# Pairwise bilinear interaction: x turned by 16 transposes a tile with straight and crosswise copies in place of 32, and three parts of w in one buffer

## The chip, the core and the metric

The kernel runs on one core of one Trainium2 chip. The metric is device time in microseconds (us) of one execution. Before the change the median of four runs is 1346.43 us (1346.36 to 1346.82).

## The reference

x (called r_inputs) holds 4,096 samples of 32 fields of 64 numbers; w holds one 64x64 matrix for each of the 496 pairs of fields i < j. All is float32. Cut to what matters:

```python
F = inputs.shape[1]                                  # 32
idx_i, idx_j = np.triu_indices(F, k=1)               # 496 pairs, i < j
vi = inputs[:, idx_i, :]                             # (4096, 496, 64)
vj = inputs[:, idx_j, :]
vidots = jnp.einsum('bpd,pde->bpe', vi, W)           # W: (496, 64, 64)
return vidots * vj                                   # (4096, 496, 64) float32
```

So for every sample and pair the field vector x_i is multiplied by the pair's own matrix, and the result element by element by x_j. The inputs are 42 MB, the output is 520 MB.

## The kernel before, in words

**Tiles and steps.** The samples are cut into 16 blocks of 256 rows, and each block into two tiles of 128 rows, a row to a partition: 32 tiles. A tile is computed in 46 steps. A step belongs to one field i and takes up to 16 of its pairs (CH), which lie side by side in w's order: its result, 128 rows by 16 pairs by 64, fills a PSUM buffer of two banks. Steps are bundled in five groups of 90 to 105 pairs (bounds, L45), and each group collects its products in one SBUF buffer `ot`, of which there are three. When a group is complete, SyncE (SP) issues one output transfer for it (L266), of 2.9 to 3.4 MB.

**A step on the engines.** TensorE (PE) multiplies x of field i, turned so that its 64 numbers lie along the partitions (`xT`), by the turned w of the pairs (`wT`), in two matmuls, h = 0 and h = 1, for the two halves of the 64 output columns (L244). Both use 64 partitions: the halves of `wT` for the two h lie on partitions 0 to 63 and 64 to 127, so field i's turned x is needed on the lower 64 partitions for h = 0 and on the upper 64 for h = 1. Where a step's pairs cross from one part of w to the next (at pairs 128, 256 and 384), it takes four matmuls. VectorE (DVE) then multiplies the result by x of the fields j and writes `ot` (L261). For the first step of the fields 1, 3, ... 13 (`aside`) ScalarE (ACT) copies the result to `tmp` instead (L258), and GpSimd (POOL) multiplies (L259).

**Turning x.** `turn_x` (L138) turns eight fields of a tile at a time (RUN), so four times a tile. The x buffer of a block has 65 slots of 64 columns: one of zeros in front, set by POOL (L72), and 64 for the fields of the two tiles. Each transpose takes two neighbouring slots, 128 rows by 128 columns: after it field n-1 lies on the lower partitions and field n on the upper ones. One transpose is done for every field, eight a turn (L143), into a PSUM buffer `ptx`, and one ACT copy of 128x1024 takes them to `xT` (L147). A step of field i then reads its lower half from the transpose of field i+1 and its upper half from that of field i (L243, L246). So the turn of fields 8q to 8q+7 is first needed by the steps of field 8q-1.

**Turning w.** The 496 matrices are loaded in three parts of 128 and one of 112 (`load_w`, L113); the first two borrow `ot` buffers and the fourth reuses the third's. Each part is put in order in four pieces (`order_w`, L120, on DVE, POOL or ACT) and turned on PE (`turn_w`, L127), and each turned piece is copied to the part's own buffer wT (L136). Part 0 is turned ahead of the first step, the others between steps.

**Order of the work.** The program runs through one list of steps (`sched`, L167). The first three tiles (LEAD) run group by group, all three through group 0, then through group 1, and so on, so that work can begin while parts of w are still to be turned; the other 29 tiles run one after the other. A table of due places (L176 to L187) says ahead of which step each turn stands: that of x stands AHEAD = 4 places before the first step that reads it. On each engine the instructions run in the order in which the program issues them. Four PSUM buffers are shared by the steps and by all turns; there are four buffers for xT and four for tmp, which also holds the ordered w.

**Loading x.** Block 0 is loaded in two halves (one per tile) and block 1 in one piece, all by SP among the first loads of w: block 0's first half, w parts 0 and 1, block 0's second half, w part 2, block 1 (L193 to L200). Later blocks are loaded at the seventh step (LATE = 6) of the block before, by ACT's queue, and every third one by `load_fifteen` (L95): 120 rows by two transfers that POOL issues, each followed by a tiny one to the buffer `scratch` (L92), and the last 8 rows by ACT.

Of the kernel before, what the change touches and what calls it, by code (L numbers as in the profile page):

```python
# [8 lines left out]
F32 = mybir.dt.float32  # L9
# [3 lines left out]
def kernel(  # L13
# [16 lines left out]
    nc = tc.nc  # L30

    B, F, D = x.shape
    P = 128
    NB = 2
# [3 lines left out]
    E2 = D // 2  # L38
    BANK = 512
    CH = BANK // E2  # L40
    RUN = 2 * BANK // P
    p0 = [i * (F - 1) - i * (i - 1) // 2 for i in range(F)]


# [7 lines left out]
    wrows = list(zip(cuts[:-1], cuts[1:]))  # L52

    const = ctx.enter_context(tc.tile_pool(name="const", bufs=1))
    xpool = ctx.enter_context(tc.tile_pool(name="xpool", bufs=2))
    xtpool = ctx.enter_context(tc.tile_pool(name="xtpool", bufs=4))
    tpool = ctx.enter_context(tc.tile_pool(name="tpool", bufs=4))
    opool = ctx.enter_context(tc.tile_pool(name="opool", bufs=3))
    psum = ctx.enter_context(tc.tile_pool(name="psum", bufs=4, space=bass.MemoryType.PSUM))

    ident = const.tile([P, P], F32, tag="ident", name="ident")
    make_identity(nc, ident)

    xs = {}

    def rows_of(dram: bass.AP, blk: int) -> bass.AP:
        return dram[blk * NB * P : (blk + 1) * NB * P]

    def new_x(blk: int):

        xs[blk] = xpool.tile([P, 1 + NB * F, D], F32, tag="xs", name=f"xs_{blk}")
        nc.gpsimd.memset(xs[blk][:, 0, :], 0.0)  # L72

    def load_x(blk: int, eng, k0: int = 0, k1: int = NB):
        src = rows_of(x, blk).rearrange("(p k) f d -> p (k f) d", k=NB)
        eng.dma_start(out=xs[blk][:, 1 + k0 * F : 1 + k1 * F, :], in_=src[:, k0 * F : k1 * F, :])

# [8 lines left out]
    def turn_engines(k: int):  # L86
        n = k if k > 1 else 17
        c = used[0] % 8
        used[0] += 1
        src = x[: NB * n].rearrange("(p k) f d -> p k f d", k=NB)  # L90
        tc.keep_in_program_order(
            nc.gpsimd.dma_start(out=scratch[:n, :, c : c + 1], in_=src[:, :, 0, 0:1])  # L92
        )

    def load_fifteen(blk: int):  # L95
        rows = rows_of(x, blk).rearrange("(p k) f d -> p k f d", k=NB)
        dst = xs[blk][:, 1:, :].rearrange("p (k f) d -> p k f d", k=NB)
        for a, b in ((SWR, SWR + 5), (SWR + 5, P)):
            nc.scalar.dma_start(out=xs[blk][a:b, 1:, :], in_=rows[a:b].rearrange("p k f d -> p (k f) d"))
        for h in range(2):  # L100
            cut = slice(h * F // 2, (h + 1) * F // 2)
            tc.keep_in_program_order(
                nc.gpsimd.dma_start(out=dst[:SWR, :, cut, :], in_=rows[:SWR, :, cut, :])  # L103
            )
            turn_engines(1)
# [3 lines left out]
    raw, wT = {}, {}  # L109
    EU = 2 * BANK // P  # L110
    NU = E2 // EU

    def load_w(c: int, eng=nc.sync):  # L113

        a, b = wrows[c]
        pool, tag = ((opool, "ot"), (opool, "ot"), (const, "w3"), (const, "w3"))[c]
        raw[c] = pool.tile([P, D * D], F32, tag=tag, name=f"raw_{c}")
        eng.dma_start(out=raw[c][: b - a, :], in_=wflat[a:b])

    def order_w(c: int, k: int, copy):  # L120
        r = wrows[c][1] - wrows[c][0]
        rp = tpool.tile([P, EU, 2, D], F32, tag="tmp", name=f"rp_{c}_{k}")
        src = raw[c][:r, :].rearrange("p (d h e) -> p e h d", h=2, d=D)
        copy(rp[:r], src[:, k * EU : (k + 1) * EU])  # L124
        return rp

    def turn_w(c: int, k: int, rp, copy):  # L127
        r = wrows[c][1] - wrows[c][0]
        if c not in wT:
            wT[c] = const.tile([P, r, E2], F32, tag=f"w{c}", name=f"wT_{c}")  # L130
        pt = psum.tile([P, EU, P], F32, tag="ps", name=f"ptw_{c}_{k}")
        for n in range(EU):
            nc.tensor.transpose(  # L133
                pt[:, n, :r], rp[:r, n].rearrange("p h d -> p (h d)"), ident[:r, :r]
            )
        copy(wT[c][:, :, k * EU : (k + 1) * EU], pt[:, :, :r].rearrange("p e r -> p r e"))  # L136

    def turn_x(blk: int, k: int, q: int, copy):  # L138

        pt = psum.tile([P, RUN, P], F32, tag="ps", name=f"ptx_{blk}_{k}_{q}")  # L140
        for n in range(RUN):
            s = k * F + q * RUN + n
            nc.tensor.transpose(  # L143
                pt[:, n, :], xs[blk][:, s : s + 2, :].rearrange("p f d -> p (f d)"), ident
            )
        xT = xtpool.tile([P, RUN, P], F32, tag="xT", name=f"xT_{blk}_{k}_{q}")
        copy(xT, pt)  # L147
        return xT


# [8 lines left out]
    first = {}  # L159
# [11 lines left out]
    place = {ts: n for n, ts in enumerate(sched)}  # L171


    AHEAD = 4
    due: dict = {}
    for t in range(NT):  # L176
        for q in range(F // RUN):
            at = place[t, first[q * RUN - 1] if q else 0] - AHEAD
            due.setdefault(max(0, at), []).append(("x", t // NB, t % NB, q))
    for c, orders, turns in (  # L180
# [10 lines left out]
    loads[place[LEAD, LATE]] = 2  # L191

    new_x(0)  # L193
    load_x(0, nc.sync, 0, 1)
    load_w(0)
    load_w(1)
    load_x(0, nc.sync, 1, NB)
    load_w(2)
    new_x(1)
    load_x(1, nc.sync)  # L200
    turn_engines(5)

    v, p, a = nc.vector.tensor_copy, nc.gpsimd.tensor_copy, nc.scalar.copy
    xT, rps = {}, {}
    xT[0, 0, 0] = turn_x(0, 0, 0, a)
    due[0] = [d for d in due[0] if d != ("x", 0, 0, 0)]
    for k, copy in enumerate((v, v, v, a)):
        rps[0, k] = order_w(0, k, copy)
    for k, copy in ((0, a), (3, a), (1, v), (2, a)):
        turn_w(0, k, rps.pop((0, k)), copy)  # L210

    ots = {}
    for s, (t, st) in enumerate(sched):
        blk, kt = divmod(t, NB)
        g, i, c0, m = steps[st]
        if s in loads:
            new_x(loads[s])
            if loads[s] % 3 == 1:
                load_fifteen(loads[s])
            else:  # L220
                load_x(loads[s], nc.scalar)
        for what, *args in due.get(s, ()):
            if what == "x":
                xT[tuple(args)] = turn_x(*args, a)
            elif what == "turn":
                turn_w(*args, rps.pop(tuple(args)), a)
            else:
                c, k = args
                rps[c, k] = order_w(c, k, (v, v, p, v)[c] if k % 2 == 0 else (v, v, p, a)[c])
                if (c, k) == (2, NU - 1):  # L230
                    load_w(3, nc.scalar)

        base, end = groups[g]
        pa = p0[i] + c0
        if pa == base:
            ots[t] = opool.tile([P, cap, D], F32, tag="ot", name=f"ot_{t}_{g}")
        ot = ots[t]
        ps = psum.tile([P, 2, CH, E2], F32, tag="ps", name=f"ps_{s}")
        for c, (lo, hi) in enumerate(wrows):
            lo, hi = max(pa, lo), min(pa + m, hi)  # L240
            if lo < hi:
                for h in range(2):
                    n = i + 1 - h  # L243
                    nc.tensor.matmul(  # L244
                        ps[:, h, lo - pa : hi - pa, :],
                        xT[blk, kt, n // RUN][h * D : (h + 1) * D, n % RUN, :],  # L246
                        wT[c][h * D : (h + 1) * D, lo - wrows[c][0] : hi - wrows[c][0], :],
                        start=True,
                        stop=True,
                    )  # L250
        o = pa - base
        j = 1 + kt * F + i + 1 + c0
        dst = ot[:, o : o + m, :].rearrange("p m (h e) -> p m h e", h=2)
        src = ps[:, :, :m, :].rearrange("p h m e -> p m h e")
        xj = xs[blk][:, j : j + m, :].rearrange("p m (h e) -> p m h e", h=2)
        if i in aside and c0 == 0 and s not in no_aside:
            tmp = tpool.tile([P, CH, 2, E2], F32, tag="tmp", name=f"tmp_{s}")
            nc.scalar.copy(tmp, src)  # L258
            nc.gpsimd.tensor_mul(dst, tmp, xj)  # L259
        else:  # L260
            nc.vector.tensor_mul(dst, src, xj)  # L261

        ends = (p0[2], end) if s < NS and (t, g) == (0, 0) else (end,)
        if pa + m in ends:
            n0 = p0[2] if len(ends) > 1 and pa + m == end else base
            nc.sync.dma_start(  # L266
                out=rows_of(out, blk).rearrange("(p k) n d -> p k n d", k=NB)[:, kt, n0 : pa + m, :],
                in_=ot[:, n0 - base : pa + m - base, :],
            )
# [28 lines left out]
```

## Time and profile before

| | before |
|---|---|
| median of 4 runs | 1346.43 us (1346.36 to 1346.82) |
| the profiled execution: its time | 1346.36 us |
| its span | 1344.6 us |
| PE busy | 1164.9 us, 87% of the span |
| DVE busy | 955.6 us, 71% |
| POOL busy | 544.9 us, 41% |
| ACT busy | 374.1 us, 28% |
| moved by DMA | 562.95 MB, mean 419 GB/s |

The page gives, for one profiled execution, the busy time of each engine; the span cut into 40 slices of 33.6 us with a digit each for the busy share in tenths, for the granted clock of PE, and for the 16 DMA engines together; the DMA queues (q1 is what SP issues, q10 what ACT issues, q0 what POOL issues, q8 the fetching of instructions); the chain of waits, followed back from the last instruction; and the costliest groups of instructions. A row of a group reads: line, engine, operation, output <- inputs and their shapes, how many | busy us, mean ns of one | idle us of the engine just before them, and what ended most of that. PE's matmuls are pipelined: the mean length of one is longer than the distance from one to the next. Busy shares say little alone: an engine that waits for the transfers can be busy for most of the span. What tells is which wait ends last in each stretch, so the trace is also read in short windows of time and as a timeline of one engine after the other.

### The profile page before, as it was taken

What the parts mean: (1) busy time and instruction counts of PE and PEld (TensorE: products, weight loads), DVE (VectorE), ACT (ScalarE), POOL (GpSimd) and SP (SyncE); (2) the same over time, 40 slices, a digit from 0 to 9 for tenths busy, and PEclk for the clock granted to TensorE, in tenths of its full rate; (3) what the DMA queues carried; (4) which work ended last, traced back from release to release, by engine and by line L of the source; (5) the groups of instructions that cost most, each with busy time, mean ns of one, the idle gap of its engine ahead of it and who ended that gap; (6) DMA issues with size and microseconds to landing.
All of it is one profiled execution on the core that took longest, in us unless ns stands there. A gap on an engine that the chain in (4) does not pass through costs nothing.

```text
span 1344.6 us, 17902 instructions
## 1 busy us (share of the span) xinstructions
PE 1164.9 (87%) x7424; PEld 681.4 (51%) x7424; DVE 955.6 (71%) x1262; ACT 374.1 (28%) x367; POOL 544.9 (41%) x264
## 2 busy tenths in 40 slices
PE   6989889888898888888889988888988879889894
PEld 4556545545455454455445554454554445545552
DVE  4778767766677677776757777576776767767774
ACT  3432222223232232232222322222232323223321
POOL 1813433444243445333434434442444424344431
PEclk9989999999999899998989999899899989989997
DMA  9999999999999999999999999999999999999997
GB/s 385 373 421 420 416 429 431 429 421 428 422 431 420 432 430 403 426 424 431 431 415 424 410 426 429 421 432 417 415 427 413 431 420 425 422 428 430 423 417 320
DMA packets 28258, 562.95 MB, mean 419 GB/s; under 512 B 3456, under 2 KB 3456, under 8 KB 5504
## 3 DMA queue, kind: packets, MB, share of 16 engines
q1 hardware_dynamic: 24048, 530.59, 93.0%
q10 hardware_dynamic: 1632, 23.33, 4.2%
q0 software_dynamic: 2496, 7.88, 1.5%
q8 instruction: 58, 0.95, 0.3%
q14 instruction: 24, 0.20, 0.0%
HBM read 41.68 MB, written 520.09 MB: 418 GB/s over the span
## 4 chain that ended last, share of the span: by engine, by line
DMA 50%; PE 24%; DVE 16%; POOL 5%; issue 2%; ACT 1%; DVEq 0%; SPq 0%; POOLq 0%; ACTq 0%
DMA out_dram<-ot 49%; PE ps L244 19%; DVE ot L261 16%; POOL ot L259 4%; PE ptx L143 4%; PE ptw L133 1%; DMA raw<-in_L_rec_W_dram 1%; ACT tmp L258 1%; DVE rp L124 0%; POOL scratch L92 0%; POOL xs L103 0%; POOL rp L124 0%; DVEq L261 0%; ACT wT L136 0%; POOLq L259 0%
## 5 line engine op out<-in xcount | busy, mean ns | idle before, releaser
L261 DVE TENSOR_TENSOR ot<-ps,xs 128x1024 f32<-128x1024 f32 (+15 forms) x1252 | 944.3, 808 | 357.3 <-DMA out_dram<-ot 187.6
L244 PE MATMUL ps<-wT,xT 64*128 64x512 f32 (+13 forms) x6272 | 1019.0, 467 | 122.1 <-DVE ot L261 110.4
L244 PEld LDWEIGHTS ps<-wT,xT 64*128 64x128 f32 x6272 | 554.1, 194 | 552.5 <-DVE ot L261 288.5
L259 POOL TENSOR_TENSOR ot<-tmp,xs 128x1024 f32<-128x1024 f32 x220 | 519.2, 2360 | 622.8 <-ACT tmp L258 442.0
L258 ACT COPY tmp<-ps 128x1024 f32<-128x1024 f32 x220 | 222.7, 1012 | 468.9 <-PE ps L244 401.7
L147 ACT COPY xT<-ptx 128x1024 f32<-128x1024 f32 x128 | 129.6, 1012 | 451.0 <-PE ptx L143 451.0
L143 PE MATMUL ptx<-ident,xs 128*128 128x128 f32 x1024 | 141.2, 281 | 36.0 <-DVE ot L261 27.2
L143 PEld LDWEIGHTS ptx<-ident,xs 128*128 128x128 f32 x1024 | 111.2, 142 | 82.6 <-issue 42.3
L72 POOL MEMSET xs<- 128x64 f32 x16 | 2.4, 151 | 148.4 <-DVE ot L261 148.4
L133 PE MATMUL ptw<-ident,rp 128*128 128x128 f32 (+1 forms) x128 | 19.0, 304 | 3.9 <-DVE rp L124 3.9
L133 PEld LDWEIGHTS ptw<-ident,rp 128*128 128x128 f32 (+1 forms) x128 | 16.1, 160 | 10.3 <-DVE rp L124 5.0
L136 ACT COPY wT<-ptw 128x1024 f32<-128x1024 f32 (+1 forms) x15 | 14.8, 984 | 21.3 <-PE ptw L133 21.3
L124 DVE COPY rp<-raw 128x1024 f32<-128x1024 f32 (+1 forms) x9 | 10.7, 1212 | 11.3 <-DMA raw<-in_L_rec_W_dram 11.3
L92 POOL DMA_DIRECT2D scratch<-in_r_inputs_dram x10 | 9.1, 908 | 0.2 <-issue 0.2
L124 POOL COPY rp<-raw 128x1024 f32<-128x1024 f32 x4 | 7.9, 1975 | 0.1
L124 ACT COPY rp<-raw 112x1024 f32<-112x1024 f32 (+1 forms) x3 | 5.9, 1958 | 4.7 <-POOL ot L259 2.9
L103 POOL DMA_DIRECT2D xs<-in_r_inputs_dram x8 | 6.0, 754 | 1.4 <-issue 1.4
L136 DVE COPY wT<-ptw 128x1024 f32<-128x1024 f32 x1 | 1.2, 1225 | 3.1 <-PE ptw L133 3.1
L147 ACT ACT_TABLE_LOAD x1 | 1.3, 1283 | 0.7 <-PEq L285 0.7
masks.py:197 POOL MEMSET ident<- 128x128 f32 x1 | 0.2, 204 | 0.3 <-POOLq L285 0.3
masks.py:199 POOL TENSOR_SCALAR_AFFINE_SELECT ident<-ident 128x128 f32<-128x128 f32 x1 | 0.3, 287 | 0.0
L285 POOL MEMSET const-float32-0.0<- 128x1 f32 x1 | 0.1, 93 | 0.3 <-issue 0.3
(3 smaller groups left out, 0.3 us busy)
## 6 DMA issues: line engine op xcount, KB each, us to landing
out_dram<-ot SPq DMA_DIRECT2D x64, 3360.0 KB, 16.3
out_dram<-ot SPq DMA_DIRECT2D x32, 3168.0 KB, 16.4
out_dram<-ot SPq DMA_DIRECT2D x32, 3104.0 KB, 17.0
out_dram<-ot SPq DMA_DIRECT2D x31, 2880.0 KB, 17.1
xs<-in_r_inputs_dram ACTq DMA_DIRECT2D x10, 2048.0 KB, 18.5
xs<-in_r_inputs_dram POOLq DMA_DIRECT2D x8, 960.0 KB, 31.8
raw<-in_L_rec_W_dram SPq DMA_DIRECT2D x3, 2048.0 KB, 17.6
xs<-in_r_inputs_dram SPq DMA_DIRECT2D x2, 1024.0 KB, 5.6
```

Of the source, the lines that this page charges most:

```text
L72: nc.gpsimd.memset(xs[blk][:, 0, :], 0.0)
L92: nc.gpsimd.dma_start(out=scratch[:n, :, c : c + 1], in_=src[:, :, 0, 0:1])
L103: nc.gpsimd.dma_start(out=dst[:SWR, :, cut, :], in_=rows[:SWR, :, cut, :])
L124: copy(rp[:r], src[:, k * EU : (k + 1) * EU])
L133: nc.tensor.transpose(pt[:, n, :r], rp[:r, n].rearrange("p h d -> p (h d)"), ident[:r, :r])
L136: copy(wT[c][:, :, k * EU : (k + 1) * EU], pt[:, :, :r].rearrange("p e r -> p r e"))
L143: nc.tensor.transpose(pt[:, n, :], xs[blk][:, s : s + 2, :].rearrange("p f d -> p (f d)"), ident)
L147: copy(xT, pt)
L244: nc.tensor.matmul(ps[:, h, lo - pa : hi - pa, :], xT[blk, kt, n // RUN][h * D : (h + 1) * D, n % RUN, :], wT[c][h * D : (h + 1) * D, lo - ...
L258: nc.scalar.copy(tmp, src)
L259: nc.gpsimd.tensor_mul(dst, tmp, xj)
L261: nc.vector.tensor_mul(dst, src, xj)
```

## The change

The x buffer loses its column of zeros, and with it POOL's memset. `turn_x` transposes only the pairs of fields (8q, 8q+1), (8q+2, 8q+3) and so on: four transposes instead of eight, into half as large a PSUM buffer. After them even fields lie on the lower partitions and odd ones on the upper. xT now has two planes: plane 0 takes the transposes as they are (one copy of 128x512), and plane 1 takes them crosswise, the lower 64 partitions of the transposes to the upper ones of xT and the upper to the lower (two copies of 64x512). A step of field i reads plane (i+h) % 2: for an even field plane 0 has the lower half and plane 1 the upper, and for an odd one the other way round. The turn of fields 8q to 8q+7 is now first needed by the steps of field 8q itself, and stands AHEAD = 6 places before that. The first three parts of w are turned into one buffer of 384 pairs, so that a step needs four matmuls only where it crosses pair 384.

```diff
-    RUN = 2 * BANK // P
+    RUN = 8
...
-        xs[blk] = xpool.tile([P, 1 + NB * F, D], F32, tag="xs", name=f"xs_{blk}")
-        nc.gpsimd.memset(xs[blk][:, 0, :], 0.0)
+        xs[blk] = xpool.tile([P, NB * F, D], F32, tag="xs", name=f"xs_{blk}")
...
     def turn_w(c: int, k: int, rp, copy):
         r = wrows[c][1] - wrows[c][0]
-        if c not in wT:
-            wT[c] = const.tile([P, r, E2], F32, tag=f"w{c}", name=f"wT_{c}")
+        home, tag, n = (wrows[c][0], "w3", r) if c == 3 else (0, "w", wrows[3][0])
+        if home not in wT:
+            wT[home] = const.tile([P, n, E2], F32, tag=tag, name=f"wT_{home}")
...
-        copy(wT[c][:, :, k * EU : (k + 1) * EU], pt[:, :, :r].rearrange("p e r -> p r e"))
+        o = wrows[c][0] - home
+        copy(wT[home][:, o : o + r, k * EU : (k + 1) * EU], pt[:, :, :r].rearrange("p e r -> p r e"))
 
     def turn_x(blk: int, k: int, q: int, copy):
 
-        pt = psum.tile([P, RUN, P], F32, tag="ps", name=f"ptx_{blk}_{k}_{q}")
-        for n in range(RUN):
-            s = k * F + q * RUN + n
+
+        pt = psum.tile([P, RUN // 2, P], F32, tag="ps", name=f"ptx_{blk}_{k}_{q}")
+        for u in range(RUN // 2):
+            s = k * F + q * RUN + 2 * u
             nc.tensor.transpose(
-                pt[:, n, :], xs[blk][:, s : s + 2, :].rearrange("p f d -> p (f d)"), ident
+                pt[:, u, :], xs[blk][:, s : s + 2, :].rearrange("p f d -> p (f d)"), ident
             )
-        xT = xtpool.tile([P, RUN, P], F32, tag="xT", name=f"xT_{blk}_{k}_{q}")
-        copy(xT, pt)
+        xT = xtpool.tile([P, 2, RUN // 2, P], F32, tag="xT", name=f"xT_{blk}_{k}_{q}")
+        copy(xT[:, 0], pt)
+        copy(xT[D:, 1], pt[:D])
+        copy(xT[:D, 1], pt[D:])
         return xT
...
-    AHEAD = 4
+    AHEAD = 6
     due: dict = {}
     for t in range(NT):
         for q in range(F // RUN):
-            at = place[t, first[q * RUN - 1] if q else 0] - AHEAD
+            at = place[t, first[q * RUN]] - AHEAD
             due.setdefault(max(0, at), []).append(("x", t // NB, t % NB, q))
...
-        for c, (lo, hi) in enumerate(wrows):
-            lo, hi = max(pa, lo), min(pa + m, hi)
+        for lo, hi in ((0, wrows[3][0]), wrows[3]):
+            home, lo, hi = lo, max(pa, lo), min(pa + m, hi)
             if lo < hi:
                 for h in range(2):
-                    n = i + 1 - h
                     nc.tensor.matmul(
                         ps[:, h, lo - pa : hi - pa, :],
-                        xT[blk, kt, n // RUN][h * D : (h + 1) * D, n % RUN, :],
-                        wT[c][h * D : (h + 1) * D, lo - wrows[c][0] : hi - wrows[c][0], :],
+                        xT[blk, kt, i // RUN][h * D : (h + 1) * D, (i + h) % 2, i % RUN // 2, :],
+                        wT[home][h * D : (h + 1) * D, lo - home : hi - home, :],
                         start=True,
                         stop=True,
                     )
```

The remaining lines of the change follow from the lost column: the x buffer is addressed from slot 0 in the loads (L76, L97, L99) and in the multiplies (L252).

More of the change, by code (lines that the diff above doesn't have):

```diff
@@ L69, in new_x @@
     def new_x(blk: int):
-        xs[blk] = xpool.tile([P, 1 + NB * F, D], F32, tag="xs", name=f"xs_{blk}")
-        nc.gpsimd.memset(xs[blk][:, 0, :], 0.0)
+        xs[blk] = xpool.tile([P, NB * F, D], F32, tag="xs", name=f"xs_{blk}")
     def load_x(blk: int, eng, k0: int = 0, k1: int = NB):
         src = rows_of(x, blk).rearrange("(p k) f d -> p (k f) d", k=NB)
-        eng.dma_start(out=xs[blk][:, 1 + k0 * F : 1 + k1 * F, :], in_=src[:, k0 * F : k1 * F, :])
+        eng.dma_start(out=xs[blk][:, k0 * F : k1 * F, :], in_=src[:, k0 * F : k1 * F, :])
     SWR = 120
@@ L96, in load_fifteen @@
         rows = rows_of(x, blk).rearrange("(p k) f d -> p k f d", k=NB)
-        dst = xs[blk][:, 1:, :].rearrange("p (k f) d -> p k f d", k=NB)
+        dst = xs[blk].rearrange("p (k f) d -> p k f d", k=NB)
         for a, b in ((SWR, SWR + 5), (SWR + 5, P)):
-            nc.scalar.dma_start(out=xs[blk][a:b, 1:, :], in_=rows[a:b].rearrange("p k f d -> p (k f) d"))
+            nc.scalar.dma_start(out=xs[blk][a:b], in_=rows[a:b].rearrange("p k f d -> p (k f) d"))
         for h in range(2):
@@ L251 @@
         o = pa - base
-        j = 1 + kt * F + i + 1 + c0
+        j = kt * F + i + 1 + c0
         dst = ot[:, o : o + m, :].rearrange("p m (h e) -> p m h e", h=2)
```

## The prediction, made before the result was known

> **What bounds the kernel now.** I read the page first: its span, busy shares and slices, and its DMA queues.
>
> ```profile
> span 1344.6 us, 17902 instructions
> PE 1164.9 (87%) x7424; PEld 681.4 (51%) x7424; DVE 955.6 (71%) x1262; ACT 374.1 (28%) x367; POOL 544.9 (41%) x264
> DMA  9999999999999999999999999999999999999997
> q1 hardware_dynamic: 24048, 530.59, 93.0%
> q8 instruction: 58, 0.95, 0.3%
> ```
>
> PE is busy for 87% of the span, but the transfers fill nine tenths or more of every slice but the last. The costliest groups, with what ended the idle time before them, say who waits for whom:
>
> ```profile
> L261 DVE TENSOR_TENSOR ot<-ps,xs 128x1024 f32<-128x1024 f32 (+15 forms) x1252 | 944.3, 808 | 357.3 <-DMA out_dram<-ot 187.6
> L147 ACT COPY xT<-ptx 128x1024 f32<-128x1024 f32 x128 | 129.6, 1012 | 451.0 <-PE ptx L143 451.0
> L143 PE MATMUL ptx<-ident,xs 128*128 128x128 f32 x1024 | 141.2, 281 | 36.0 <-DVE ot L261 27.2
> ```
>
> DVE idles 187.6 us until an output transfer frees a buffer: in the long run compute waits for the transfers. Third, short stretches of time (columns: length; PE, PEld, DVE, ACT, POOL busy; PE clock; DMA share; GB/s):
>
> ```profile
> 35.00:36.00 1.00, 1.00 (x6) 0.49 (x6) 0.75 (x1) 0.83 (x1) 0.94 (x2) 1.00 0.07 30
> 103.00:104.00 1.00, 1.00 (x11) 0.64 (x8) 1.00 (x3) 0.43 (x1) 0.44 (x1) 1.00 0.06 25
> 1337.00:1338.00 1.00, 0.00 (x0) 0.00 (x0) 0.00 (x0) 0.00 (x0) 0.00 (x0) 0.50 0.06 27
> 1341.00:1342.00 1.00, 0.00 (x0) 0.00 (x0) 0.00 (x0) 0.00 (x0) 0.00 (x0) 0.50 0.06 27
> ```
>
> A share of 0.06 is one of sixteen DMA engines working alone. The last 5 us of the span belong to one that has fallen behind, and when the others ran dry at 35 and 103 us it alone still had work. So: work saved on any compute engine in the steady part gives nothing. The time moves if an output issue comes so late that even this engine runs dry, or if its own work becomes faster or slower. At 35 us it is nearly dry: the issue of tile 1's first group at 35.81 restarts everything.
>
> **The change, part by part.** The profiled execution took 1346.36 us, 1.8 more than its span, and stands 0.07 below the median of 1346.43; the sum is made on 1346.4.
>
> *Transposes, matmuls.* 512 of 1,024 transposes go; eight back to back take 1.09 us in the timeline below, so 512 take 70 us off PE. A step that crosses pair 128 or 256 needs two matmuls in place of four; a few us more. PE then has some 1,090 us of 1,345. Cover: the transfers. Worth 0. If there were no cover, PE's 24% of the chain of waits bounds what it could be; it would show at 80 to 104 us, where the chain runs through PE, but of that stretch only one turn (0.55 saved) lies on it, and there the lagging engine is still fed.
>
> *ScalarE copies.* Each turn's one copy of 1,012 ns becomes one of 512 columns and two crosswise ones of half the partitions. From the row of 1,012 ns for 1,024 columns and one of 906 for 896 I get 0.83 ns a column, so 588 ns for 512. No row shows half the partitions: each lies between 0 and 1,012; I take 588, as the rows vary by column. 128 x (3 x 588 - 1,012) = +96 us (ends -54 and +205), so ACT goes from 374 to 470, at most 579, 43% of the span. Cover: ACT's own idle time, 451 us ahead of these copies alone. Queued behind them on ACT are the copies to tmp that POOL waits for, and the w copies; +0.75 us on one of these is small beside POOL's 59% idle. Worth 0.
>
> *The column of zeros, POOL's queue.* 16 memsets of 151 ns go, with their 148.4 us of waiting for the old x buffer. The four POOL transfers of a block loaded over fifteen engines come, by the order of POOL's queue, behind the block's first multiply instead of ahead of it: up to one multiply (2.36 us) later, for transfers wanted more than a tile (some 42 us) on, landing in 31.8. Worth 0. Output issues on SP keep their order, and so does DVE.
>
> *The head.* AHEAD goes from 4 to 6, and a first turn is placed by its own step: in PE's order the turn of tile 2's fields 0 to 7 moves from before the ninth step to before the seventh. It reads x block 1, the last of the six input loads. In the timeline of before it comes at 29.64 (start, length, engine, line):
>
> ```profile
> 21.14 1.09 PE L143 MATMUL ptx<-ident,xs 128*128 128x128 f32 x8
> 25.00 2.69 PE L244 MATMUL ps<-wT,xT 64*128 64x512 f32 x12
> 27.61 1.09 PE L133 MATMUL ptw<-ident,rp 128*128 128x128 f32 x8
> 28.64 1.08 PE L244 MATMUL ps<-wT,xT 64*128 64x480 f32 x4
> 29.64 1.09 PE L143 MATMUL ptx<-ident,xs 128*128 128x128 f32 x8
> 32.60 3.15 DVE L261 TENSOR_TENSOR ot<-ps,xs 128x896 f32<-128x896 f32 x3 [0.71 <-PE ps L244]
> ```
>
> The issues of all six loads are over at 4.03 us, and together they are 10.49 MB. By 26 us, at 389 GB/s over the stretch from 0, 10.1 MB are through; at 267 to 328 GB/s the rest takes 1.3 us, and with the lagging engine and the notice I put the landing at 28.0 to 28.5. The trace has no landing for this load; the bounds are 27.3 and 29.6, where PE finds it landed. In after, tile 1's turn (21.14) has moved ahead of the first step, into the wait for w that ends at 19.28, and PE is through its sixth step at about 25.5. It then stands until 28.0 to 28.5, and behind it, in order, steps seven to twelve and two turns of w. From 28.5: turn 0.55, step 1.0, turn of w 1.0, step 0.95, then DVE's multiply 1.2 and its ordering copy 1.05, three multiplies 3.15: tile 1's output issue falls at 37.4 instead of 35.81, +1.6. From a landing of 27.3 it is +0.4, from 29.6 +2.7. The lagging engine, dry at about 36.7, gets its next bytes 1.5 later. Nothing behind gives this back: it has no other idle time of that size. **+1.5, ends 0 and +2.7.**
>
> *The clock.* The stall is a gap of 2.5 to 3 us on PE. A gap on PE of 2.96 us, 72.37 to 75.33, has this in the windows:
>
> ```profile
> 72.40:75.30 2.90, 0.00 (x0) 0.00 (x0) 0.79 (x2) 1.62 (x1) 0.75 (x1) 0.90 1.10 471
> 75.30:80.00 4.70, 4.42 (x19) 3.41 (x20) 4.70 (x4) 1.98 (x1) 1.60 (x1) 0.50 1.00 426
> 80.00:85.00 5.00, 4.88 (x22) 3.10 (x21) 4.24 (x6) 1.01 (x1) 0.00 (x0) 0.51 0.99 426
> 85.00:88.00 3.00, 3.00 (x23) 1.93 (x21) 1.88 (x2) 0.91 (x1) 0.00 (x0) 1.00 0.96 414
> ```
>
> After it the clock was 0.50 for nearly 10 us. Of the trace's 28 gaps of 1.9 to 4.5 us on PE, all eight of 2.9 and more were followed by half clock, 3.4 us of it or more (the one at 8.46 shows it in its transposes, one in 213 ns until 16.6 us and one in 110 from there), but only eight of the 20 between 2.0 and 2.5. If the stall triggers it, the 3.4 us of PE work behind take 1.7 more, all of it on the way to the issue at 37.4: +3.2 in all. The stall lies between the two groups. The rises of the clock, at 16.6 and 84.9 us, lie twenty times 3.41 us apart; if it is judged at such ticks, one at 26.8 cuts the stall into two short halves. I take it without.
>
> [...] No run here shows this stall yet.
>
> *Instruction fetch.* PE's records fall from 14,848 to 13,312, 10.3%. The instruction queue takes 0.3% of sixteen engines' span, 64.5 us of engine time; 10.3% of that is 6.7 us. If it all came off the lagging engine -6.7, if spread evenly -0.4; the 58 packets lie over many engines, so -0.5. Beyond it I can't say why this engine lags: it takes about 0.95 us more per tile than the others, 30 us in all, and only while compute runs. Were that in proportion to PE's instructions, 10.3% of it is -3.1.
>
> Sum: 1346.4 + 1.5 - 0.5 = **1347.4 us**.
>
> **The rivals.** *Half clock in the head (slower).* The stall tips the clock: 1346.4 + 3.2 - 0.5 = 1349.1. For it: the 2.96 us gap. Against: the shorter gaps that did not. It decides if PE's gap at 25.5 to 28.5 reaches about 2.9 us. With a landing at 29.6 it is 1350.3.
>
> *The lagging engine gets lighter (faster).* Fewer PE instructions relieve it: -3.1 with the stall's +1.5 or with none gives 1344.8 or 1343.3; if the fetches are all its own, 1341. For it: it lags only while compute runs. Against: its excess per tile is as constant in tiles with more PE work as in those with less.
>
> *Nothing arrives.* x block 1 has landed by about 27, or the engine had backlog enough at 36.7: 1346.4 - 0.5 = 1345.9, and up to 1346.4.
>
> *The change doesn't do what it says:* only if a crosswise copy between partition halves were far dearer than its row. At 2.0 us each (twice my upper end) ACT would have some 830 us, still covered.
>
> **How the numbers follow.** Stall at full clock 0.36, half clock 0.33, lighter engine 0.16, nothing 0.15. The likeliest gives 1347.4. The range runs from 1344.0 (most of the lighter engine's cases with the stall) to 1350.0 (nearly all of the half clock); about 0.1 is left out on either side. A measurement of this kernel can tell some 0.2%, 2.7 us, from no change: faster is below 1343.7, slower above 1349.1. The stall and nothing at all lie within; half clock lies on the upper bound, and as a later landing makes both the stall and the fall longer, 0.27 of its 0.33 lie above it; of the lighter engine 0.12 lies below. Faster 0.12, same 0.61, slower 0.27.
>
> **What would show it.** Right: a wait of PE for x at about 25.5 us that ends near 28, an output issue near 37.4 instead of 35.81, the same shift at the end, and one DMA engine alone from about 1338 on. Copies of three times about 0.6 us, ACT near 470 us, PE near 1,090, DVE's wait for output transfers as long as before. The clock between 28 and 33 us tells the first case from the second. I am wrong if the head is unchanged and the end isn't, or if the last engine's alone time at the end is no longer 5 us: then that engine's rate has changed, and not its start.

## The result and the profile after

The changed kernel is a little faster: 1344.16 us median (1341.93 to 1345.66) against 1346.37 for the kernel before on the same chips (1345.01 to 1347.66), a ratio of 0.9984 with a 95% interval of 0.9979 to 0.9988. I had forecast 1347.4, a small loss within what can be told. The stall that I had put my money on came, where and when I had said, but on balance it left the changed kernel only 0.4 us late; a term that I had put at 0.5 us gave 3.3.

The page of the changed kernel, its first lines, the DMA queues and the copies that replace the old one:

```profile
span 1341.7 us, 16692 instructions
PE 1135.3 (85%) x6656; PEld 603.5 (45%) x6656; DVE 953.5 (71%) x1262; ACT 467.9 (35%) x623; POOL 542.3 (40%) x248
q1 hardware_dynamic: 24048, 530.59, 93.1%
q8 instruction: 52, 0.85, 0.2%
...
L264 DVE TENSOR_TENSOR ot<-ps,xs 128x1024 f32<-128x1024 f32 (+15 forms) x1252 | 940.2, 807 | 357.0 <-DMA out_dram<-ot 214.5
L149 ACT COPY xT<-ptx 128x512 f32<-128x512 f32 x128 | 75.0, 586 | 329.8 <-PE ptx L145 329.8
L151 ACT COPY xT<-ptx 64x512 f32<-64x512 f32 x128 | 74.6, 582 | 1.6
L150 ACT COPY xT<-ptx 64x512 f32<-64x512 f32 x128 | 73.9, 577 | 1.5
```

The limits are where they were: the output queue is at 93%, and DVE waits for output buffers even longer (214.5 us against 187.6), because compute has more time to spare. The copies cost what I had worked out: 586, 582 and 577 ns against 588 each. Here half the partitions take no less time than all of them.

The head, in the timeline of the changed kernel (start, length, engine, line; in brackets the idle time before and what ended it):

```profile
27.50 9.83 SPq L269 DMA_DIRECT2D out_dram<-ot  x3
27.96 0.42 PEld L145 LDWEIGHTS ptx<-ident,xs 128*128 128x128 f32 x4 [3.43 <-DVE ot L264]
27.99 0.63 PE L145 MATMUL ptx<-ident,xs 128*128 128x128 f32 x4 [2.79 <-DMA xs<-in_r_inputs_dram]
28.55 1.13 PE L247 MATMUL ps<-wT,xT 64*128 64x512 f32 x4
```

The first row merges three output issues. The third of them, tile 1's, stands alone in a narrower window, first of the kernel before, then of the changed one:

```profile
35.81 0.33 SPq L266 DMA_DIRECT2D out_dram<-ot  x1
37.00 0.33 SPq L269 DMA_DIRECT2D out_dram<-ot  x1
```

PE stands 2.79 us for x block 1 and goes on at 27.99; tile 1's issue falls at 37.00 instead of 35.81. The windows show the clock and the end (length; PE, PEld, DVE, ACT, POOL busy; clock; DMA share; GB/s):

```profile
25.00:30.00 5.00, 2.21 (x14) 1.11 (x13) 4.69 (x5) 1.32 (x3) 0.53 (x1) 1.00 0.72 304
30.00:35.00 5.00, 5.00 (x29) 2.51 (x28) 4.25 (x5) 2.45 (x3) 1.24 (x1) 1.00 0.99 411
...
36.00:37.00 1.00, 1.00 (x6) 0.52 (x8) 0.94 (x2) 0.95 (x1) 0.94 (x2) 1.00 0.07 30
...
1336.00:1337.00 1.00, 0.00 (x0) 0.00 (x0) 0.00 (x0) 0.00 (x0) 0.00 (x0) 0.50 0.06 27
1338.00:1339.00 1.00, 0.00 (x0) 0.00 (x0) 0.00 (x0) 0.00 (x0) 0.00 (x0) 0.50 0.06 27
1339.00:1340.00 1.00, 0.00 (x0) 0.00 (x0) 0.00 (x0) 0.00 (x0) 0.00 (x0) 0.50 0.00 0
```

The stall stays at full clock. The same single engine (0.06 of sixteen, 27 GB/s) still ends the run, but its last packet is through at 1339.6 us, where before it was 1342.45. It works alone for 3.7 us instead of 5, which the prediction had named as the sign that its rate, and not its start, has changed.

So the gain must lie in that engine's pace. It can be followed packet by packet: the third group's output has packets of a size that no other transfer has (25,344 bytes), and away from the blocks loaded by `load_fifteen` the last of them in each tile belongs to the lagging engine. From one tile's last to the next tile's it took, as the median of ten tiles without a load of x, 38.97 us before and 38.87 after. The packets of the five groups take 855, 921, 940, 996 and 996 ns (medians, the same before and after), eight of each a tile and engine, 37.66 us laid end to end. In the trace each starts 3 to 4 ns before the one ahead of it has ended, and an engine whose packets all take these medians (below: undisturbed) takes 37.56 us a tile: this is the period in the few tiles where such an engine ends last (37.57 us in one tile of the changed kernel, 37.56 in five of the last run below). The lagging engine takes 1.4 us a tile more before and 1.3 more after. At the first tile's end that can be compared, about 181 us, the changed kernel is still 0.42 us late (181.36 against 180.94). By 1326 us it is 2.88 us early (1323.62 against 1326.50). It gains 3.30 us on the way, about 0.1 a tile, unevenly only around the blocks that `load_fifteen` loads.

### The profile page after: what moved, and what is told of

It is laid out like the page before. It is cut to its first block, busy times and chain, and to the rows that moved or that the text cites. A ratio compares the mean times of both kernels' runs of the same rounds, so it can differ in the third digit from the quotient of the medians.

```text
span 1341.7 us, 16692 instructions
## 1 busy us (share of the span) xinstructions
PE 1135.3 (85%) x6656; PEld 603.5 (45%) x6656; DVE 953.5 (71%) x1262; ACT 467.9 (35%) x623; POOL 542.3 (40%) x248
## 4 chain that ended last, share of the span: by engine, by line
DMA 60%; PE 18%; DVE 13%; POOL 4%; issue 2%; ACT 1%; SPq 0%; DVEq 0%; POOLq 0%; ACTq 0%
DMA out_dram<-ot 58%; PE ps L247 16%; DVE ot L264 13%; POOL ot L262 4%; DMA xs<-in_r_inputs_dram 2%; PE ptx L145 1%; ACT tmp L261 1%; PE ptw L133 1%; DVE rp L123 0%; POOL rp L123 0%; DVEq L264 0%; SPq L117 0%; SPq L75 0%; ACT xT L151 0%; ACT xT L149 0%
## 5 line engine op out<-in xcount | busy, mean ns | idle before, releaser
L264 DVE TENSOR_TENSOR ot<-ps,xs 128x1024 f32<-128x1024 f32 (+15 forms) x1252 | 940.2, 807 | 357.0 <-DMA out_dram<-ot 214.5
L247 PE MATMUL ps<-wT,xT 64*128 64x512 f32 (+13 forms) x6016 | 1043.4, 487 | 162.3 <-DVE ot L264 157.6
L262 POOL TENSOR_TENSOR ot<-tmp,xs 128x1024 f32<-128x1024 f32 x220 | 519.1, 2360 | 772.6 <-ACT tmp L261 583.2
L247 PEld LDWEIGHTS ps<-wT,xT 64*128 64x128 f32 x6016 | 532.9, 194 | 614.3 <-DVE ot L264 364.5
L149 ACT COPY xT<-ptx 128x512 f32<-128x512 f32 x128 | 75.0, 586 | 329.8 <-PE ptx L145 329.8
L145 PE MATMUL ptx<-ident,xs 128*128 128x128 f32 x512 | 85.1, 290 | 21.5 <-DVE ot L264 10.1
L145 PEld LDWEIGHTS ptx<-ident,xs 128*128 128x128 f32 x512 | 54.5, 142 | 94.2 <-DVE ot L264 72.6
L151 ACT COPY xT<-ptx 64x512 f32<-64x512 f32 x128 | 74.6, 582 | 1.6
L150 ACT COPY xT<-ptx 64x512 f32<-64x512 f32 x128 | 73.9, 577 | 1.5
## 6 DMA issues: line engine op xcount, KB each, us to landing
xs<-in_r_inputs_dram POOLq DMA_DIRECT2D x8, 960.0 KB, 30.5
```

The lines of the kernel that those rows point to most:

```text
L145: nc.tensor.transpose(pt[:, u, :], xs[blk][:, s : s + 2, :].rearrange("p f d -> p (f d)"), ident)
L149: copy(xT[:, 0], pt)
L150: copy(xT[D:, 1], pt[:D])
L151: copy(xT[:D, 1], pt[D:])
L247: nc.tensor.matmul(ps[:, h, lo - pa : hi - pa, :], xT[blk, kt, i // RUN][h * D : (h + 1) * D, (i + h) % 2, i % RUN // 2, :], wT[home][h * ...
```

## The experiments

**Theory.** Every instruction that the engines run costs the lagging DMA engine a fixed time, so fewer instructions make its pace. **Rivals:** the gain comes from POOL's lost memsets and its moved transfers; from PE's shorter time on the path; or from the data that PE reads from SBUF.

The table has what the runs gave; the texts of what was expected follow. Instructions are from each page's first line, "at 181" and "period" are the lagging engine's times as above. The ratio is to the kernel before on the same chip, with its 95% interval. "ns each" is the period less the 37.56 us of an undisturbed engine, divided by the instructions of one tile, a thirty-second of the page's number.

```
kernel                          instr.  at 181   period  ns each  ratio to before
before                          17902   180.94   38.97    2.52
after                           16692   181.36   38.87    2.51    0.9984 (0.9979-0.9988)
transposes twice                17716   181.36   38.95    2.51    1.0002 (0.9992-1.0011)
small matmuls on PE             18719   183.04   39.04    2.53    1.0041 (1.0026-1.0056)
small copies on ACT             17661   182.97   38.98    2.57    1.0004 (0.9995-1.0013)
before, w in one buffer         17390   180.76   38.93    2.52    0.9988 (0.9978-0.9998)
after, first turns moved back   16721   179.07   38.91    2.58    0.9965 (0.9952-0.9977)
 and w cut at 376               16465   187.13   38.86    2.53    1.0027 (1.0017-1.0037)
 and cut at 376, full-row loads 16465   180.81   38.87    2.55    0.9969 (0.9958-0.9980)
```

**The transposes twice.** The same work done twice puts PE instructions back, with their time and their data, and leaves the other engines' work as it is.

```diff
-        for u in range(RUN // 2):
+        for u in (0, 1, 2, 3, 0, 1, 2, 3):
```

> The changed kernel with each of its four transposes of a turn done twice into the same place (the first result is overwritten): 512 transposes and 512 weight loads more on PE, 14,336 records against 13,312 and against 14,848 of before; ACT, POOL and DVE as in the changed kernel. Theory (the lagging DMA engine is slowed by each PE instruction): before, its excess was about 0.95 us a tile, 30 us in all, over 14,848 PE records, some 2.05 ns a record; 1,024 records cost +2.1 us, so 1346.2 us against 1344.1, and the engine's period per plain tile goes from 38.87 to about 38.94 us. Rival (the gain came from POOL's lost memsets, from the moved loads, or from ACT): nothing comes back, 1344.1. Rival (the gain is PE time on the path, at the head): part of the turn's 0.55 us at the head comes back, at most 1 us, and the period per tile stays.

The median is 1346.65 us, 1.0002 of before: the gain is gone in the medians, and 0.08 of the 0.10 us in the period are back. In the profiled execution the engine is at 181.36 us as in the changed kernel (that it agrees to the hundredth is chance: output issues lay up to 3 us later in between), and 1.66 us behind it at 1325.28; its time, 1345.17 us, is 1.66 more than the 1343.51 of the changed kernel's. This is less than the 2.6 us of 1,024 instructions at 2.5 ns, mainly because two tiles loaded by `load_fifteen` went 0.5 and 0.7 us faster than in the changed kernel. So the head is not the cause of the faster pace, and neither are the memsets, the moved transfers or ACT's copies, which are all as in the changed kernel.

**Small matmuls.** Instructions that move next to no data:

```diff
+            for _ in range(TINY):                      # TINY = 1
+                nc.tensor.matmul(pt[:, u, 0:1], lhsT=ident, rhs=ident[:, 0:1], start=True, stop=True)
             nc.tensor.transpose(
```

> The changed kernel with one matmul of a single column from the identity ahead of each transpose, into the place that the transpose overwrites: 512 small matmuls, by the records of other float32 matmuls 1,024 records and as many weight loads, +2,048 on PE, with next to no data moved through PE's inputs and outputs. Theory (the number of PE instructions): 2,048 x 2.05 ns = +4.2 us, about 1348.3 us, period per plain tile about 39.0. Rival (what slows the engine is the SBUF data that PE reads, the 128x128 columns of the transposes): 0, 1344.1, while the doubled transposes come back to 1346. Rival (PE's time on the path): under 1 us.

The period goes to 39.04, above that of the kernel before, and the engine loses 4.22 us between 181 and 1326 us against the changed kernel. So it isn't the 128x128 data of the transposes. Another 1.7 us are lost by 181 us, but not to the stall: tile 1's issue falls at 36.40, 0.6 us before that of the changed kernel, and the issues fall behind only later, by 5.5 us at 148 us. I take this to be PE's added time, which nothing covers there; no run tests it. The profiled execution took 1349.44 us, 5.93 more than the changed kernel's, which is just these two (4.22 + 1.68 = 5.90); the median of four, 1352.4, lies 3 us above it, and I can't say why.

**Small copies on ACT.** Whether it is PE's instructions or all:

```diff
+        for u in range(8):
+            copy(xT[:, 0, u % 4, 0:1], pt[:, u % 4, 0:1])
         copy(xT[:, 0], pt)
```

> The changed kernel with eight copies of one column each on ACT ahead of every turn's straight copy, which overwrites them: 1,024 more ACT instructions, none more on PE. Theory (PE's instructions alone): the period per plain tile stays at 38.87 and the time at 1344.1, but for up to 0.5 us at the head, where each turn's copies end some 1.5 us later. Rival (instructions of any engine count alike): 1,024 x 2.05 ns = +2.1 us, 1346.2, period 38.94.

The rival holds: 1,024 instructions on ACT slow the engine as those on PE do, period 38.98, and 2.58 us are lost between 181 and 1326 us. A queue of instruction packets, q14, grows with ACT's count too. It has 24 packets before, with 367 ACT instructions; in the changed kernel, with 623, and here:

```profile
q14 instruction: 26, 0.21, 0.0%
q14 instruction: 34, 0.28, 0.0%
```

Eight packets of 8,192 bytes more for 1,024 instructions are 64 bytes for each (an estimate from these two rows). The run also shows something that I had as a rival of the prediction. Its stall in the head tipped the clock; in its timeline and windows:

```profile
28.17 1.11 PE L145 MATMUL ptx<-ident,xs 128*128 128x128 f32 x4 [2.28 <-DVE ot L266]
29.21 2.08 PE L249 MATMUL ps<-wT,xT 64*128 64x512 f32 x4
```

```profile
28.00:30.00 2.00, 1.83 (x6) 1.22 (x8) 2.00 (x3) 0.65 (x9) 0.00 (x0) 0.51 0.59 250
30.00:32.00 2.00, 2.00 (x10) 0.78 (x7) 0.78 (x2) 1.71 (x3) 0.00 (x0) 0.64 0.90 375
32.00:34.00 2.00, 2.00 (x12) 1.05 (x12) 1.16 (x2) 1.01 (x1) 0.00 (x0) 1.00 1.03 430
```

A gap of 2.28 us before the turn, and four matmuls take 2.08 us where they took 1.13. From the turn to the second step behind it PE needs 4.17 us (28.17 to 32.34), where the changed kernel needs 2.64 (27.99 to 30.63): the half clock costs 1.5 us, where I had put 1.7 on it. Tile 1's issue falls at 38.71 instead of 37.00, and 1.6 us of this are left at 181 us.

So the two cases of the stall are both real, and it is the longer gap that kept the full clock. The granted clock in the traces shows what half clock went with. In the traces of the kernels before and after, the changes of the clock lie whole numbers of 3.413 us apart, as on a grid. From 27 to 1300 us of these two, a slot of this grid that ran at full clock was followed by half clock in all 45 cases in which PE stood idle for 2.0 us or more of it, in none of 615 with less than 1.6 us, and in 4 of 23 between. A grid point at 26.69 us cuts the changed kernel's gap into 1.49 and 1.30 us; here 2.15 of the 2.28 us lie in one slot, 24.62 to 28.04. The grid lay elsewhere in each of the three (a point at 26.91 us before, at 26.69 after, at 24.62 and 28.04 here), so the full clock of the changed kernel's profile may have been luck: if every position is equally likely, a gap of 2.79 us would put 2.0 us or more into one slot in about two executions of three (an estimate from the 3.413 and the 2.0 us).

**The stall alone.** The first turn of a tile goes back to its old place, everything else stays:

```diff
-            at = place[t, first[q * RUN]] - AHEAD
+            at = place[t, first[q * RUN]] - (AHEAD if q else 4)
```

> The changed kernel with the turns of a tile's first eight fields back at four places before their step, where the kernel before has them; the other turns stay at six. PE's gap of 2.8 us at 25.2 us goes, and tile 1's first output issue falls at about 35 us instead of 37.00. Theory (the head's delay lives to the end): 1.2 us at the issue, of which the output that ends at 181 us still showed 0.4 against before: -0.4 to -1.2, about 1343.3 us. Rival (the head's delay is made good by 104 us, where the transfers wait for PE in either kernel): 0, 1344.1.

The median is 1341.63 us (1341.12 to 1342.64), ratio 0.9965. That is 0.19% of 1346, 2.5 us, below the changed kernel's ratio. In the timeline PE no longer waits, and the turn stands where x has long landed:

```profile
26.25 1.09 PE L133 MATMUL ptw<-ident,rp 128*128 128x128 f32 x8
27.27 1.07 PE L247 MATMUL ps<-wT,xT 64*128 64x480 f32 x4
28.27 0.66 PE L145 MATMUL ptx<-ident,xs 128*128 128x128 f32 x4
28.86 3.44 PE L247 MATMUL ps<-wT,xT 64*128 64x512 f32 x16
```

Tile 1's issue falls at 34.24, 2.76 us before that of the changed kernel and 1.57 before that of the kernel before; at 181 us 2.29 and 1.87 of this are still there. Neither expectation had it: the stall costs 2.3 us at that mark where I had 1.5, because without it the head is faster than that of the kernel before.

**w in one buffer alone,** in the kernel before, is the diff's parts in `turn_w` and in the loop over the parts of w, with nothing of x changed: 512 PE records fewer.

```diff
-        for c, (lo, hi) in enumerate(wrows):
-            lo, hi = max(pa, lo), min(pa + m, hi)
+        for lo, hi in ((0, wrows[3][0]), wrows[3]):
+            home, lo, hi = lo, max(pa, lo), min(pa + m, hi)
```

> The kernel before with the first three turned parts of w in one buffer, and nothing else changed: 256 matmuls and 256 weight loads fewer on PE, 14,336 records against 14,848. Theory (every instruction costs the lagging DMA engine about 2.6 ns, as the doubled transposes, the small matmuls and the small copies gave): 512 x 2.6 ns = -1.3 us, 1345.0 us, the engine's period per plain tile 38.91 against 38.95. Rival (merging w does nothing, the gain is all the transposes'): 1346.3 and 38.95.

1343.99 us against 1345.62, ratio 0.9988 (0.9978 to 0.9998): -1.6 us, with a period of 38.93 against 38.97. In the profiled execution 0.94 us are gained between 181 and 1326 us. The fewer matmuls pay the same 2.52 ns each (table), on their own, though PE's busy time stays the same (1165.0 us against 1164.9).

**The last split step, and a slow load.** If counts matter, the last split steps are worth removing too: w is cut at pair 376, where the steps of field 16 begin.

```diff
-    cuts = [*range(0, NP, P), NP]
+    cuts = [0, P, 2 * P, p0[16], NP]
```

> The changed kernel with the first turns back at four places before their step, and w cut at pairs 0, 128, 256 and 376 in place of 384: pair 376 is where the steps of field 16 begin, so no step needs four matmuls any more; 128 matmuls and 128 weight loads fewer on PE, 13,056 records. Theory (2.6 ns an instruction): 256 x 2.6 = -0.7 us against the kernel with only the turns moved back, so about 1341.0 us, period 38.85. Rival (counts do not matter this finely, or the longer fourth part of w costs the head more than this): 1341.6 or above.

1349.24 us, ratio 1.0027 against 0.9965 without the cut, some 8 us worse. The period is as expected (38.86); the loss is all there at 181 us (187.13 against 179.07). The windows of this kernel, and then of the one without the cut:

```profile
20.00:24.00 4.00, 4.00 (x25) 2.00 (x22) 3.86 (x4) 2.44 (x4) 0.00 (x0) 1.00 0.98 213
24.00:28.00 4.00, 4.00 (x25) 2.13 (x25) 3.94 (x5) 1.35 (x3) 2.36 (x1) 1.00 0.92 209
```

```profile
20.00:24.00 4.00, 4.00 (x24) 2.27 (x24) 4.00 (x5) 3.03 (x5) 0.20 (x1) 1.00 1.02 434
24.00:28.00 4.00, 4.00 (x24) 1.94 (x20) 3.94 (x4) 1.37 (x2) 2.17 (x1) 1.00 0.97 412
```

The DMA engines are as busy and move half as much. The third part of w is now a load of 120 rows. Its packets of 16 KB took a median of 1,268 ns instead of 611, it landed at 28.30 us instead of 22.87, and PE waited 4.2 us for x block 1 behind it. The next run keeps the cut and loads 128 rows:

```diff
-        eng.dma_start(out=raw[c][: b - a, :], in_=wflat[a:b])
+        for lo, hi in {2: ((a, a + P),), 3: ((a, a + 112), (a + 112, b))}.get(c, ((a, b),)):
+            eng.dma_start(out=raw[c][lo - a : hi - a, :], in_=wflat[lo:hi])
```

> As the run with w cut at pair 376, with the third part's load kept at 128 rows (the last eight of them unused) and the fourth part's 120 rows loaded as 112 and 8. In that run the window from 20 to 28 us, with the load of 120 rows of w under way, moved 209 to 213 GB/s against 412 to 434 with 128 rows, and the third part landed at 28.30 us instead of 22.87. Theory (the lost 7 us are that load, and the cut itself saves 256 instructions at 2.6 ns): the third part lands at about 23 us, tile 1's first output issue is at 34.3 again, and the time is 0.7 us below that of the kernel with only the turns moved back, about 1341.0. Rival (the longer fourth part costs the head 7 us): 1348.

1341.41 us, ratio 0.9969, and 180.81 at the first mark instead of 187.13: the loss is gone, and the third part's packets take 611 ns again, so it was the load. This run also splits the fourth part's load; but that comes at 55 us, and the third part's lateness is there by 28 us. Why 120 rows ran so slowly is not shown. The cut's own -0.7 us can't be told: against 0.9965 without the cut the intervals overlap. The head lost 1.7 us at 181 us to the run without it, and the engine gained 1.0 of that by 1326 us.

**More blocks by `load_fifteen`.** It takes load off the lagging engine: before, a tile with such a load takes 41.8 to 42.1 us by the last packets, others with a load 43.7. How many engines carry it the trace doesn't record. It was tried with every second block in place of every third, first with the slow load still in:

```diff
-            if loads[s] % 3 == 1:
+            if loads[s] % 2 == 1:
```

> As the run with w cut at pair 376 and the first turns moved back, and every second block's x loaded over fifteen engines (blocks 3, 5, ... 15, seven of them) in place of every third (four). At the end of the changed kernel the lagging engine works alone for some 4 us. Theory (it alone sets the end): a block loaded over fifteen engines costs it 1.3 to 1.9 us less over its two tiles; three more blocks give -4 to -5.7 us for it, of which the others' lead of 4 us less what they take over allows about -3: 1338 us, and the stretch of one engine alone at the end about 0 to 1 us. Rival (POOL's issuing and its place behind multiplies delay the loads, or all engines slow down together): no gain or a loss, 1341 to 1344 us.

1349.12 us, ratio 1.0022 against 1.0027: no difference that can be told, with the slow load still in both. Without the slow load, with the cut and then without it:

> The same with every second block's x over fifteen engines. Theory (the lagging engine alone sets the end, 4 us alone in the kernel with only the turns moved back): from 188 to 1291 us the earlier pair of runs differed by 1.1 us in favour of every second block, so about 1340 us, and the engine's stretch alone at the end under 2 us. Rival (the other engines are the bound by then, as the stretch alone was only 1 us in either of the earlier pair): no difference, 1341.

> The changed kernel with the first turns back at four places and every second block over fifteen engines, w cut as in the changed kernel. Theory: 1 to 3 us below the same with every third block, 1339 to 1340.5 us. Rival (the other engines take over the end, or POOL's loads come later): 1341.6 or above.

1340.18 and 1340.17 us, ratios 0.9959 (0.9944 to 0.9974) and 0.9955 (0.9939 to 0.9972). The end of the run without the cut, in windows, and below it the same two windows with every third block:

```profile
1334.00:1335.00 1.00, 0.00 (x0) 0.00 (x0) 0.00 (x0) 0.00 (x0) 0.00 (x0) 0.50 0.19 81
1335.00:1336.00 1.00, 0.00 (x0) 0.00 (x0) 0.00 (x0) 0.00 (x0) 0.00 (x0) 0.50 0.19 81
```

```profile
1334.00:1335.00 1.00, 0.00 (x0) 0.00 (x0) 0.00 (x0) 0.00 (x0) 0.00 (x0) 0.50 0.06 27
1335.00:1336.00 1.00, 0.00 (x0) 0.00 (x0) 0.00 (x0) 0.00 (x0) 0.00 (x0) 0.50 0.06 27
```

Three engines (0.19) share the last stretch, where one alone worked for 3 us with every third block. So the lagging engine no longer sets the end by itself, and what is left to gain is small, as the rival had it: each run is about 1 us, 0.1%, below its partner with every third block, inside the intervals. Both are clearly below the kernel before, by 5.5 us. The changed kernel with the first turns moved back is the simplest of the versions that beat it and the kernel before.

## Why the prediction was right and wrong

**The step that failed: "Instruction fetch", -0.5.** I worked from the 0.3% of the instruction queue and the 58 packets that lie over many engines, and put the rest, "I can't say why this engine lags", aside with a bound of -3.1 that went into a rival at a chance of 0.16. That rival was the case: -3.30 us between 181 and 1326 us. The doubled transposes bring 0.08 of the 0.10 us in the period back; the small matmuls and copies raise it by their number, on either engine. My reason against it, that the excess is as constant in tiles with more PE work as in those with less, was no argument: the plain tiles have the same number of instructions, all of them.

How well a plain count does is in the column "ns each". In all nine kernels, whose instructions differ by 14%, the lagging engine's excess over an undisturbed engine is 2.51 to 2.58 ns an instruction: it is in proportion to the count, with nothing fitted. The prediction had put this excess at 0.95 us a tile, against all the other engines; against an undisturbed one it is 1.4. The 64 bytes by which q14 grew for each ACT instruction would take 2.4 ns at the 27 GB/s that the engine moves alone (an estimate from these two numbers), nearly its excess for each instruction; that it carries such bytes is not shown. What is shown is that its period follows the number of PE's and of ACT's instructions: the three runs that add them to the changed kernel lengthen it by 0.08, 0.17 and 0.11 us. DVE's and POOL's were not varied, and what slows the engine stays open. It is not the 16 KB packets of the instruction queue as the trace records them: periods with one such packet and periods with two are alike (38.87 in the changed kernel). The extra comes instead in small portions on nearly every packet, 33 ns a packet on the mean after and 35 before: its eight of 25,344 bytes up to 263.88 us after took 940 to 992 ns, seven of them more than the median of 940. Every run here was recorded, so whether it is the recording of instructions itself can't be excluded.

**The head: the stall was right, its sum was half right.** The place (the turn of tile 2's first fields, behind x block 1), the length (2.79 us; 2.5 to 3 forecast), the restart at 27.99 (28.0 to 28.5) and the full clock were as told. The issue came at 37.00, forecast 37.4, so +1.19 instead of +1.6. "Nothing behind gives this back" was wrong: tile 2's issue was late by 0.77 us only, and at 181 us 0.42 were left. The step behind this is "Transposes, matmuls: worth 0", whose cover, the transfers, isn't there in the head. With the stall taken out, the same lighter PE puts the issue 1.57 us ahead of the kernel before and keeps 1.87 at 181 us. What I priced as a stall of 1.5 is one of 2.3 less 1.9 of saved work, which left +0.4.

**The sum against the measured parts,** by the profiled executions: +0.4 (forecast +1.5) in the head, -3.3 (forecast -0.5) in the pace: -2.9, and 1346.36 became 1343.51. The medians of many runs moved by 2.2. The half clock didn't come in the profile of the changed kernel and came in that of the small copies, so that rival is real and its price of 1.7, measured at 1.5, nearly right. Its condition, a gap of about 2.9 us, is wrong: 2.28 us were enough in that run, with 2.15 of them in one slot, and 2.79 us in the changed kernel's, split 1.49 and 1.30, were not. The prediction had this as an aside, a tick at 26.8 us that would cut the stall into two short halves, and the trace has one at 26.69; but nothing in the prediction could tell where the ticks would fall. Whether the half clock hits other executions of the changed kernel isn't settled: their times spread over 3.7 us in 32 runs, those of the kernel with the first turns moved back over 1.5 us in only six.

**The steps costed at nothing** held where I could see them: ACT went to 467.9 us (470 forecast); POOL waits longer for its copies to tmp (583.2 us against 442.0) and PE's weight loads 8.2 us in all for the last crosswise copies, but neither bounds the steady part; POOL's moved transfers landed in 30.5 us (31.8 before); the memsets' waits are gone, and no gain in the time is seen from them. PE's busy time fell to 1,135 only, not to 1,090: the transposes' row fell by 56 us (141.2 to 85.1) and not by 70, and that of the steps' matmuls, fewer but wider, rose by 24 (1019.0 to 1043.4). In the steady part nothing came of it.

## What to carry to other kernels

When transfers bound a kernel, find the one DMA engine that ends last and follow its packets from tile to tile: here a pace that differed by 0.10 us in 38.97 a tile could be read there, where the medians differ by 0.16% in all, and it moved with the number of instructions on PE and on ACT. A term that can't be explained and is as large as the gain in question deserves its own bound in the sum, not a rival's chance. And a start-up phase needs its own account: a saving that is hidden for the rest of the run can be worth its price there (1.9 us at the 181 us mark here), and an earlier place for a step is a wait if its data is the last to load (2.79 us here).

## What the runs showed that I had not expected

- One DMA engine lagged by 2.51 to 2.58 ns for each instruction of a tile in nine kernels that differ in their PE or ACT instructions: 512 PE records fewer gave 1.6 us of 1346 (interval 0.3 to 3.0).
- In these traces the half clock followed the idle time of PE in one slot of a grid of 3.413 us (2.0 us or more, 45 of 45), not the length of the gap: 2.79 us of gap kept the full clock, 2.28 lost it.
- A load of 120 rows of 16 KB, in place of 128, moved some 210 GB/s instead of 420: a packet took 1,268 ns instead of 611 (medians), while the share of busy DMA time stayed at 0.92 to 0.98. Loading eight rows that nobody reads, with the fourth part's 120 rows as 112 and 8, was 6.3 us cheaper at the 181 us mark.
- A copy of 64 partitions took as long as one of 128 on ACT: 577 to 582 ns against 586 for 512 columns.
